# Attention b's stream: the order of VectorE, ScalarE and GpSimd within a step is taken from the source, as TensorE's already is

## The chip, the cores and the metric

The kernel runs on one core of a Trainium2 chip, in one launch. The metric is the device time of one execution in microseconds (us). The engines are named as the profile names them: PE is TensorE, DVE is VectorE, ACT is ScalarE, POOL is GpSimd, and SP is the engine that issues the DMAs.

## The reference

The input `x` is float32 of shape [2][512][512]: two batches of 512 tokens with 512 features. Four layers follow one another, each with a layer norm in front and a residual around it:

```python
x = x + attn_a(layernorm(x))   # 32 heads, 8 key heads, head size 128, int4 weights
x = x + ffn(layernorm(x))      # 8 experts of rank 64, top 2 per token   ("f1")
x = x + attn_b(layernorm(x))   # 32 heads, 8 key heads, head size 16
x = x + ffn(layernorm(x))      # the same experts again                  ("f2")
```

Attention b, cut to what matters here:

```python
q, k, v = rope(resid @ Wq), rope(resid @ Wk), resid @ Wv
att = q @ k.T / sqrt(16)                     # per head, 4 heads share a key head
att = where(causal, att, -inf)
out = softmax(att) @ v
return heads_joined(out) @ Wo
```

The experts' layer, for each token: softmax of eight gates, the two largest kept and scaled to a sum of one, and `out = sum over e of w[e] * (x @ A[e].T @ B[e].T)`.

## The kernel before, in words

The whole computation is written in a scheduling framework: the source emits instructions, and a scheduler decides in what order each engine's queue holds them, from its own estimate of when they are ready. A region `with tc.manual_schedule(engines={...})` takes this freedom away for the engines that it names: each of them issues the instructions emitted inside this region in the order of emission. The order between engines stays a matter of semaphores, and where a region's instructions fall among those of the same engine that are emitted outside it (another region too) stays the scheduler's.

The tokens of a batch are four tiles of 128 rows. `x[b, t]` stays in SBUF (`x_r` in the profile), and every residual is added in place. The layers of the two batches overlap. After attention a and the first projections, one long loop, the **stream**, does attention b for both batches (L948 to L985), and beside it, as fillers, pieces of the other layers.

**The stream's main work.** It goes over 32 pairs; a pair `p` is two heads of one batch (16 pairs a batch). Each pair takes three steps, and the second half of a pair's work follows the first by eight steps (`LEAD`), so the loop has 104 steps. Each step is a region of its own, in which only PE keeps the emitted order. In a step, in order of emission:

- `queries_halved(p + 1)`, once in four pairs: it splits a block of turned queries into a rounded part (ACT, L752) and the rest (POOL, L753), tile `hl`, and sends it through DRAM (SP, L734).
- `queries_in(p)`: SP loads the pair's queries `qs` (L761), POOL clears their extra rows (L763).
- `maxima_in(p)`: PE transposes the row maxima (`tpm`, L804), and ACT copies them into the extra rows of `qs` (L807), so that the next product comes with the maximum subtracted.
- `probabilities`: PE multiplies keys by queries (`st_b`, L828), ACT takes the exponential (`pT_b`, L834), POOL clears what lies above the diagonal (affine select, L837).
- `maxima`: PE multiplies queries by keys (`sc_b`, L781), DVE takes each row's maximum from PSUM (`top`, L785); at the end of a pair POOL splits these maxima in two parts with four small operations (`mm`, L793 and L794). The tiles are taken as (0, 1), then 3, then 2, so a tile name `sc_b_2_3_0` is pair 2, tile 3, half 0.
- `weighted_b`: PE multiplies probabilities by values (`num_b`, L854); for the last tile ACT copies the result out (L865), and DMAs send its sums.

`sc_b`, `st_b` and `tpm` share five PSUM banks (pool `ps_x`), the fillers have two (`ps_f`), and `num_b` has one. A bank comes free when DVE or ACT has read what it held.

**The fillers** are Python generators that a number called `pace` advances a little in each step, at the step's end. In the first half these are the rest of experts f1 for batch 1 and `projections(1)` (norm, keys, queries of batch 1); in the second half `output_b` (the output projection `po`, L910, with its residual, L914) and experts f2 for batch 0. A filler begins with `norm_parts` (L158): for each of the four tiles the statistics and their aggregate on DVE (`bn_stats`, L163; `bn_aggr`, L164), then the standard deviation (ACT, square root, L166), its reciprocal (DVE, L168), the normalised tiles `xn` (DVE, L173), their transposes `pxT` (PE, L178), and a copy (ACT, L179). ACT's square root and exponential have different tables, so the trace has a table load ahead of L166 and another ahead of the next exponential. All of the norm's statistics are emitted in one piece:

```python
for t in range(NT):
    st = small.tile([P, 6], F32, tag="st", name=f"st_{which}_{b}_{t}")
    nc.vector.bn_stats(st, x[b, t])
    nc.vector.bn_aggr(var[:, t, :], st)
```

Of the experts, these lines matter here: for each tile POOL spreads the gate weights (`we`, L255), PE transposes them (`wT`, L259), DVE multiplies them in (L261), and then come the products `py` (PE, L266) with the residual (DVE, L270) and the store of the output (SP, L272). `divided` (L882) turns the sums into reciprocals, loads them as a broadcast (`rb`, L897, SP), and multiplies (`oN`, L900, DVE).

After the stream the rest follows on its own: the output projection of batch 1 and experts f2 for batch 1.

Of the kernel before, what the change touches and what calls it, by code (L numbers as in the profile page):

```python
# [40 lines left out]
def kernel(  # L41
# [238 lines left out]
    with ExitStack() as actx:  # L280
# [226 lines left out]
        def chain(*stages):  # L507
            for stage in stages:
                yield from stage
# [231 lines left out]
    def keys_in(b, kh):  # L741

        if kh == 0:
            kparts[b] = spread(khls[b], f"k_{b}", (slice(0, 4, 2), slice(1, 4, 2)))
        nc.sync.dma_start(ks[kh][:HALF], kparts[b][:, ts(kh, 4), :])

    def queries_halved(p):

        b, kh, g, _ = pairs[p]
        hl = hlp.tile([P, 2, S], F32R, tag="hl", name=f"hl_{p}")  # L750
        src = qTs[b][:, kh * 2 + g // 2, :]
        nc.scalar.copy(hl[:, 0, :], src)  # L752
        nc.gpsimd.tensor_tensor(hl[:, 1, :], src, hl[:, 0, :].bitcast(F32), ALU.subtract)  # L753
        to = spread(hl, f"q_{p}", (slice(0, 2), slice(2, 4)))
        for n in range(4):
            qparts[p + n] = to

    def queries_in(p):
        _, _, g, pr = pairs[p]
        q = qs[p % NQ]  # L760
        nc.sync.dma_start(q[:HALF], qparts.pop(p)[:, ts((g % 2) * 2 + pr, 2), :])  # L761
        if p >= NQ:
            nc.gpsimd.memset(q[HALF:HM], 0.0)  # L763
# [35 lines left out]
    def maxima_in(p):  # L799

        mm = mms.pop(p).bitcast(F32)
        tp = ps_x.tile([P, S], F32, tag="x", name=f"tpm_{p}")
        for t in range(NT):
            nc.tensor.transpose(tp[:HM, ts(t, P)], mm[:, t, :], ident)  # L804
        for h in range(2):
            at = (1 - h) * HALF
            nc.scalar.copy(qs[p % NQ][HALF:HM, h, :].bitcast(F32R), tp[at : at + 2, :])  # L807
# [39 lines left out]
    def weighted_b(b, kh, g, j, pT):  # L847


        first, last = j == 0, j == NT - 1  # L850
        if first:
            nums[b, kh, g] = ps_n.tile([P, S], F32, tag="num", name=f"num_b_{b}_{kh}_{g}")
        for sp in range(4):
            nc.tensor.matmul(  # L854
                nums[b, kh, g][ts(sp, STRIP), j * P :], vpads[b][:, j, kh, sp, :], pT[sp],
                start=first, stop=last,
            )
        if not last:
            return
        c, par = kh * 2 + g // 2, g % 2  # L860
        if par == 0:
            got = oNs[b, c] = bp.tile([P, S], F32, tag="oN", name=f"oN_b_{b}_{c}", bufs=6)
        else:
            got = temps.tile([P, S], F32, tag="t", name=f"o1_b_{b}_{c}")
        nc.scalar.copy(got, nums.pop((b, kh, g)))  # L865

        row, pair = (c % 2) * 2 + par, (b, kh)
        if row == 0:
            dens[pair] = dram.tile([2, 4, 2, S], F32, tag=f"dens{kh}", name=f"dens_b_{b}_{kh}", bufs=1)
        nc.sync.dma_start(dens[pair][c % 2, :, par, :], got[B_HD:P:STRIP, :])  # L870
        if par == 1:

            for sp in range(4):
                at = sp * STRIP
                nc.sync.dma_start(oNs[b, c][at + B_HD : at + STRIP, :], got[at : at + B_HD, :])
        if row == 3:
            quotients.append(divided(b, kh))
# [25 lines left out]
    def output_b(b, cs):  # L903

        while not all((b, c) in ready for c in cs):
            yield MM
        for i in range(NT):
            po = place("bank", [P, DM], f"po_{b}_{i}_{cs[0]}")
            for c in cs:
                nc.tensor.matmul(  # L910
                    po, oNs[b, c][:, ts(i, P)], wo2[:, c, :], start=(c == cs[0]), stop=(c == cs[-1])
                )
                if c == cs[-1]:
                    nc.vector.tensor_tensor(x[b, i], x[b, i], po, ALU.add)  # L914
                yield MM

    def run(*stages):
        stages = list(stages)
        while stages:
            stages = [st for st in stages if next(st, stages) is not stages]  # L920
# [25 lines left out]
    banks[:], homes["we"] = BESIDE, (wep, "we")  # L946
    side = chain(later, projections(1))
    pace, left = 0.8, 0.0  # L948
    for step in range(total + LEAD):
        with tc.manual_schedule(engines={mybir.EngineType.PE}):  # L950
            if step == LEAD:
                pace = 0.95
            if step == half - 4:
                run(side)
                keys_in(1, 0)
                queries_halved(len(pairs) // 2)
                side = output_b(0, (0, 1))
                pace, left = 0.37, 0.0
            if step == half + LEAD:
                keys_in(1, 1)  # L960
            if step == half + LEAD + 10:
                side = chain(side, output_b(0, (2, 3)), experts(0, "f2", True))
                pace, left = 0.95, 0.0
            if step == total - 6:
                side = chain(output_b(1, (0, 1)), side)
                pace, left = 1.4, 0.0
            quotients[:] = [q for q in quotients if next(q, None) is not None]
            p, at = divmod(step + 4, STEPS)
            if at == 0 and p % 4 == 3 and p + 1 < len(pairs) and p + 1 != len(pairs) // 2:
                queries_halved(p + 1)  # L970
            if at == 0 and 2 <= p < len(pairs):
                queries_in(p)
            p, at = divmod(step - 4, STEPS)
            if at == 0 and 0 <= p < len(pairs):
                maxima_in(p)
            if LEAD <= step:
                next(ps)
            if step < total:
                next(ms)

            if len(due) > 3 and due[3][0] <= step:
                for _ in range(4):
                    weighted_b(*due.pop(0)[1])
            left += pace
            while left > 0:  # L985
                got = next(side, None)
                if got is None:
                    left = 0.0
                else:
                    left -= got  # L990
# [99 lines left out]
```

## Time and profile before

| | us |
|---|---|
| median of three runs | 1094.37 (1093.66 to 1094.58) |
| profiled execution, its own time | 1095.07 |
| its span, first to last instruction | 1093.4 |

| engine | busy, us | share of the span | instructions |
|---|---|---|---|
| PE | 1046.9 | 96% | 4940 |
| DVE | 859.0 | 79% | 2175 |
| ACT | 627.2 | 57% | 1475 |
| POOL | 598.5 | 55% | 916 |

The mean granted clock of PE is 0.992 of full speed. Times in the trace count from the span's start. The stream runs from about 792 to 1028 us. In a line of the timeline, the first number is the start, the second the duration; then come engine, source line, operation, what it writes and reads, with shapes and the count that is drawn together in this line; in square brackets stands how long the engine was idle just before, and whose work ended that wait. A weight load of PE has an engine name of its own, PEld.

### The profile page before, as it was taken

The numbers are of one execution on the slowest core, as the hardware profiler recorded it, in microseconds if no ns is written. First come the engines' busy times: TensorE is split into PE (matmuls) and PEld (weight loads), VectorE is DVE, ScalarE is ACT, GpSimd is POOL, SyncE is SP. The second block draws the span as 40 slices with busy tenths as digits, with TensorE's granted clock in tenths as the row PEclk, the third lists the DMA queues.
The fourth block names the chain that finished last, engine by engine and source line by source line (L and its number), as shares of the span: only waits on it lengthen the run. The fifth ranks groups of instructions, "written<-read, shape, count | busy, mean of one in ns | idle before, by whom it ended". The sixth has DMA issues, their size and how long they took to land.

```text
span 1093.4 us, 16248 instructions
## 1 busy us (share of the span) xinstructions
PE 1046.9 (96%) x4940; PEld 707.0 (65%) x4940; DVE 859.0 (79%) x2175; ACT 627.2 (57%) x1475; POOL 598.5 (55%) x916
## 2 busy tenths in 40 slices
PE   5799999999999999999999999999999999999988
PEld 3477767777777677777777777556467655565534
DVE  6889899999999999999999999574386667766142
ACT  3666666567666566566666665513166567685410
POOL 2466666677576666666666666262245566554200
PEclk9999999999999999999999999999999999999999
DMA  7301011012110010010021000042342235211011
GB/s 294 116 1 39 1 39 39 1 39 78 39 40 25 16 39 20 20 39 12 28 75 42 1 1 1 1 155 75 87 161 83 57 122 149 88 49 35 28 38 39
DMA packets 23271, 60.47 MB, mean 55 GB/s; under 512 B 4369, under 2 KB 5329, under 8 KB 20369
## 3 DMA queue, kind: packets, MB, share of 16 engines
q1 hardware_dynamic: 23184, 59.44, 16.4%
q8 instruction: 40, 0.66, 0.2%
q14 instruction: 47, 0.38, 0.1%
HBM read 45.53 MB, written 12.85 MB: 53 GB/s over the span
## 4 chain that ended last, share of the span: by engine, by line
PE 80%; DVE 9%; ACT 4%; issue 2%; POOL 2%; DMA 2%; SPq 0%; ACTq 0%; POOLq 0%; DVEq 0%
PE sc L412 11%; PE av L445 11%; PE tp L440 6%; PE ph_f L207 5%; PE ps_q L365 5%; PE ps_o L457 5%; PE ps_o L458 5%; PE ps_q L366 4%; PE st_b L828 4%; PE py_f L266 3%; PE sc_b L781 3%; PE num_b L854 3%; PE po L910 3%; PE pq_b L701 2%; DVE r_q L372 1%
## 5 line engine op out<-in xcount | busy, mean ns | idle before, releaser
L429 POOL TENSOR_SCALAR p<-p,rden 128x128 f32<-128x128 f32 (+3 forms) x256 | 152.4, 607 | 227.0 <-DVE rden L427 167.1
L420 ACT ACTIVATE p<-sc,nmx 128x128 f32<-128x128 f32 (+3 forms) x256 | 135.8, 530 | 110.3 <-DVE nmx L415 108.7
L412 PE MATMUL sc<-kT,qT 128*128 128x128 f32 (+3 forms) x512 | 180.5, 435 | 1.7 <-ACT p L420 1.3
L372 DVE SCALAR_TENSOR_TENSOR r_q<-ps_q,s_q,r_q 128x512 f32<-128x512 f32 x192 | 143.8, 749 | 20.6 <-PE ps_q L366 16.3
L467 DVE SCALAR_TENSOR_TENSOR acc<-ps_o,s_o,acc 128x512 f32<-128x512 f32 x186 | 137.5, 744 | 19.9 <-PE ps_o L458 17.7
L785 DVE CUSTOM_DVE_ANT_0 sc_b<-sc_b,tri 128x128 f32<-128x128 f32 (+3 forms) x256 | 119.8, 517 | 42.2 <-PE sc_b L781 27.8
L445 PE MATMUL av<-pT,v 128*128 128x512 f32 (+3 forms) x512 | 148.5, 433 | 0.0
L445 PEld LDWEIGHTS av<-pT,v 128*128 128x128 f32 x512 | 96.7, 189 | 64.2 <-issue 36.2
L415 DVE CUSTOM_DVE_ANT_0 sc<-sc,tri 128x128 f32<-128x128 f32 (+3 forms) x256 | 125.9, 492 | 11.2 <-PE sc L412 10.3
L441 ACT COPY pT<-tp 128x128 f32<-128x128 f32 (+3 forms) x256 | 108.2, 423 | 46.0 <-PE tp L440 45.6
L365 PE MATMUL ps_q<-xh,w_q 128*128 128x512 f32 x256 | 121.1, 473 | 3.0 <-ACT r_v L370 1.4
L440 PE MATMUL tp<-ident,p 128*128 128x128 f32 x640 | 114.2, 274 | 3.2 <-POOL p L429 1.6
L412 PEld LDWEIGHTS sc<-kT,qT 128*128 128x128 f32 x512 | 94.9, 189 | 27.6 <-ACT p L420 6.9
L457 PE MATMUL ps_o<-ah,w_o 128*128 128x512 f32 x256 | 110.4, 431 | 1.8 <-DVE acc L467 1.2
L366 PE MATMUL ps_q<-xl,w_q 128*128 128x512 f32 x256 | 101.6, 397 | 0.0
L458 PE MATMUL ps_o<-al,w_o 128*128 128x512 f32 x256 | 101.2, 395 | 0.0
L834 ACT ACTIVATE pT_b<-st_b 128x384 f32<-128x384 f32 (+1 forms) x192 | 89.8, 529 | 17.8 <-PE st_b L828 16.7
L440 PEld LDWEIGHTS tp<-ident,p 128*128 128x128 f32 x640 | 78.5, 140 | 31.6 <-issue 8.7
L837 POOL TENSOR_SCALAR_AFFINE_SELECT pT_b<-pT_b 128x128 f32<-128x128 f32 (+1 forms) x192 | 63.4, 339 | 63.6 <-ACT pT_b L834 59.6
L387 POOL TENSOR_TENSOR r_q<-r_q,tab 128x512 f32<-128x512 f32 x64 | 82.2, 1284 | 9.1 <-DVE rs_q L384 9.1
L465 POOL TENSOR_TENSOR acc<-acc,part 128x512 f32<-128x512 f32 x62 | 80.0, 1290 | 11.5 <-ACT part L464 11.5
L388 POOL TENSOR_TENSOR qT<-r_q,rs_q 128x512 f32<-128x512 f32 x64 | 82.6, 1291 | 5.0
(179 smaller groups left out, 2062.9 us busy)
## 6 DMA issues: line engine op xcount, KB each, us to landing
codes_q<-in_q_codes_dram SPq DMA_DIRECT2D x8, 1024.0 KB
codes_o<-in_o_codes_dram SPq DMA_DIRECT2D x8, 1024.0 KB
spread_q<-hl SPq DMA_DIRECT2D x16, 512.0 KB
qs<-spread_q SPq DMA_DIRECT2D x32, 256.0 KB
x_a<-in_x_dram SPq DMA_DIRECT2D x8, 256.0 KB
codes_k<-in_k_codes_dram SPq DMA_DIRECT2D x2, 1024.0 KB
codes_v<-in_v_codes_dram SPq DMA_DIRECT2D x2, 1024.0 KB
x_r<-in_x_dram SPq DMA_DIRECT2D x8, 256.0 KB
```

Of the source, the lines that this page charges most:

```text
L365: nc.tensor.matmul(ps, w[:, c, ts(h, A_HD)], xh[b][:, c, :], start=True, stop=False)
L366: nc.tensor.matmul(ps, w[:, c, ts(h, A_HD)], xl[b][:, c, :], start=False, stop=True)
L372: nc.vector.scalar_tensor_tensor(r, ps, s, r, ALU.mult, ALU.add)
L412: nc.tensor.matmul(sc[:, :n], qT[:, ts(i, P)], kT[:, :n], start=True, stop=True)
L415: nc.vector.tensor_tensor_reduce(sc[:, :n], sc[:, :n], tri[:, S - n :], -(A_HD**-0.5), 3e38, ALU.add, ALU.min, nmx,)
L420: nc.scalar.activation(pr, sc[:, :n], AF.Exp, bias=nmx, scale=-1.0, accum_out=den[:, i % 2 : i % 2 + 1],)
L429: nc.gpsimd.tensor_scalar(prs[j], prs[j], rden[:, j % 2 : j % 2 + 1], 1.0, ALU.mult, ALU.mult)
L440: nc.tensor.transpose(tp[:, j, :], prs[i][:, ts(j, P)], ident)
L445: nc.tensor.matmul(av[:, j * P :], v[:, j, :], pT[:, j, j * P :], start=(j == 0), stop=(j == NT - 1))
L457: nc.tensor.matmul(ps, w[:, h, ts(n, P)], ah, start=True, stop=False)
L458: nc.tensor.matmul(ps, w[:, h, ts(n, P)], al, start=False, stop=True)
L467: nc.vector.scalar_tensor_tensor(to, ps, s, to, ALU.mult, ALU.add)
```

## The change

The region of each of the 104 steps names four engines in place of one. DVE, ACT and POOL thereby keep the emitted order within a step; from step to step they stay free, as PE does. No instruction is added or taken away.

```diff
     side = chain(later, projections(1))
     pace, left = 0.8, 0.0
+    STREAM = {getattr(mybir.EngineType, e) for e in ("PE", "DVE", "Activation", "Pool")}
     for step in range(total + LEAD):
-        with tc.manual_schedule(engines={mybir.EngineType.PE}):
+        with tc.manual_schedule(engines=STREAM):
             if step == LEAD:
                 pace = 0.95
```

## The prediction

> **What bounds the kernel now.** I read the page's busy row first, then the windows over the stretch in which the change acts (about 780 to 1029 us), then the timeline wherever TensorE (PE) stands idle there.
>
> ```profile
> PE 1046.9 (96%) x4940; PEld 707.0 (65%) x4940; DVE 859.0 (79%) x2175; ACT 627.2 (57%) x1475; POOL 598.5 (55%) x916
> ```
>
> PE is busy 96% of the span; the other engines cost time only where they make PE wait. The windows' columns are length, busy time of PE, PEld, DVE, ACT and POOL with counts, granted clock, DMA share, GB/s:
>
> ```profile
> 782.00:808.00 26.00, 23.15 (x89) 12.90 (x87) 19.78 (x70) 8.55 (x14) 7.94 (x18) 1.00 0.53 173
> 806.00:808.00 2.00, 0.65 (x4) 0.41 (x3) 1.41 (x8) 1.97 (x3) 1.84 (x5) 1.00 0.01 4
> 808.00:840.00 32.00, 31.91 (x209) 23.90 (x210) 21.27 (x89) 23.25 (x55) 17.23 (x52) 0.95 0.23 71
> 809.00:812.00 3.00, 3.00 (x10) 2.31 (x10) 2.44 (x7) 2.94 (x7) 2.26 (x5) 0.50 0.93 320
> 962.00:1000.00 38.00, 35.89 (x222) 23.47 (x226) 27.14 (x117) 27.66 (x55) 18.98 (x57) 0.96 0.18 52
> 966.00:969.00 3.00, 3.00 (x15) 2.58 (x14) 1.57 (x9) 2.59 (x6) 1.27 (x4) 0.50 0.03 8
> 1000.00:1029.00 29.00, 28.96 (x184) 16.33 (x177) 7.74 (x23) 15.67 (x32) 10.85 (x35) 1.00 0.03 7
> ```
>
> In 808 to 840 and 1000 to 1029 PE is full: whatever delays it ahead of them reaches the end, as there is no idle time in which to win it back. It has spare time in two places, around 806 and 962, and behind each it runs some 3.4 us at half clock. These are the places where a layer norm's pieces meet the maxima. The timeline of the first:
>
> ```profile
> 787.98 0.70 DVE L163 BATCH_NORM_STATS2 st_b<-x_r 128x6 f32<-128x512 f32 x1
> 791.41 0.70 DVE L163 BATCH_NORM_STATS2 st_b<-x_r 128x6 f32<-128x512 f32 x1
> ...
> 805.90 1.27 POOL L753 TENSOR_TENSOR hl<-qT,hl 128x512 fp32r<-128x512 f32 x1 [0.23 <-ACT hl L752]
> ...
> 806.37 0.14 DVE L785 DVE_READ_ACCUMULATOR2_ANT top<- 128x1 f32 x1
> ...
> 807.45 1.28 ACT L834 ACT_TABLE_LOAD   x1
> ...
> 808.06 0.63 PE L804 MATMUL tpm<-ident,mm 128*66 128x128 f32 x4 [1.39 <-POOL mm L794]
> ```
>
> Two of the four statistics ran 15 to 20 us ahead, while DVE had nothing else; the third (798.68) and fourth (803.48) were slipped in later. The last maximum of pair 2 is read by 806.51; POOL splits it (four operations, 807.12 to 808.00) after the subtraction of `hl`; PE had waited 1.39 for that. Both table loads (1.28 each) ran before that, under the wait.
>
> **The change part by part.** It adds and removes no instruction, DMA or table load. A region is one step, so each engine keeps the emitted order within a step and is still free across steps. In the built queues of the two programs, SP's order is the same; the queues differ in five places.
>
> **A, second norm of attention b (802 to 818).** All four statistics pairs now stand between pair 2's maxima. Each costs 0.58 to 0.61 (start to start) and its aggregate 0.09. Before the last maximum lie four statistics and three aggregates, 4 x 0.59 + 3 x 0.09 = 2.63, where 0.76 lay before (803.39 to 804.06, and 0.09 at 804.66). Taking the one at 798.68 out of pair 1 brings the start forward some 0.2 (PE's wait for `mm` at 802.30 then binds). The maximum is ready 2.63 - 0.76 - 0.2 = 1.7 later, at 808.2. POOL's `hl` subtraction, now behind two selects, whose exps have moved ahead of ACT's `hl` copy, ends at 808.36 instead of 807.17. The four splitting operations take 0.88: 809.24, and `tpm_2` starts at 809.3 instead of 808.06, +1.24.
> Then ACT: the Exp reload moves behind the two `qs_2` copies (1.16). 809.95 + 1.16 + 1.28 = 812.4 for the next exp (`pT_0_3`), instead of 810.82. That is +1.6, and PE's matmuls after it need its PSUM banks; between them PE and DVE now hand over banks one by one, about 0.3 more. The first `num` group, 818.46 in the trace, starts at 820.35 at full clock (+1.9). But the trace already shows clock 0.50 behind a 2 us stretch with 0.65 busy, and the new stall is longer; with the half-clock stretch falling as it does now over this group's scores I reach 821.5, **+3.0**, and take that. Bounds: +1.2 (`tpm_2` alone, all else hidden), and +4.7 (a second half-clock stretch: 3.4 us at half speed do 1.7 us of work).
>
> One page speaks to the reload. The Trainium skill, "ScalarE: Activation LUTs", section What ACT_TABLE_LOAD costs, puts a switch of tables at 1283 ns plus about 1380 ns of drain. The trace shows the load, 962.99 to 964.27, and the next exp at 964.28, so 1.28 and no drain; by the page the reload would add 1.38 more, and A would be +4.4.
>
> **B, the norm of experts f2, batch 0 (958 to 971).** Before, the statistics are at 945.13, 950.18, 953.00 and 959.16; the last delays pair 25's maxima, and PE waits:
>
> ```profile
> 960.80 0.73 PE L781 MATMUL sc_b<-ks,qs 128*128 128x512 f32 x2 [0.69 <-DVE top L785]
> ...
> 964.83 0.33 PE L781 MATMUL sc_b<-ks,qs 128*128 128x128 f32 x1 [0.43 <-ACT pT_b L834]
> 965.32 0.61 PE L781 MATMUL sc_b<-ks,qs 128*128 128x128 f32 x3 [0.16 <-ACT pT_b L834]
> 966.38 1.06 PE L804 MATMUL tpm<-ident,mm 128*66 128x128 f32 x4
> ```
>
> Now all four stand between pair 25's maxima. They start about 0.6 earlier (the 959.16 one gone), a reciprocal and small waits leave (0.5), 2.63 comes in: 963.90 + 2.63 - 0.6 - 0.5 = 965.4. Half of the splitting follows, so `tpm_25` comes at about 966.0, which is 0.4 before the trace's 966.38, as `pxT_0` no longer precedes it. The two table loads, now on either side of the `qs_0` copies, put the next exp at 966.6 + 1.16 + 1.28 = 969.05 against 968.66; `xn` and the transposes `pxT_0`, `pxT_1` (0.35 each) come behind it. The `num` group at 970.52 starts at 970.5 at full clock (0), at 971.7 with the half-clock stretch the trace has here: **+1.2**. Bounds: -0.7 (the 0.69 wait goes and all else hides) and +2.0 (+1.7 of half clock on +0.3).
>
> **C, the end of the stream (1024 to 1030).** GpSimd's copies `we_0`, `we_1` (L255, 0.61 each) ran early, at 999.77 and 1000.71. They now come behind the selects of `pT_31`, and the transposes `wT` on PE need them:
>
> ```profile
> 1024.36 0.67 POOL L837 TENSOR_SCALAR_AFFINE_SELECT pT_b<-pT_b 128x128 f32<-128x128 f32 x2 [0.38 <-ACT pT_b L834]
> 1024.64 0.60 PE L259 MATMUL wT_f<-ident,we_f 128*128 128x128 f32 x4
> 1025.31 0.61 POOL L255 COPY we_f<-gw_f 128x512 f32<-128x512 f32 x1 [0.27 <-PE wT_f L259]
> ...
> 1026.07 2.36 PE L854 MATMUL num_b<-pT_b,vpad 128*32 128x512 f32 x32
> ```
>
> `we_0` ends at 1025.0 + 0.6 = 1025.6, so `wT_0` starts at 1025.65 instead of 1024.64. `we_1` stands behind the two 0.4 selects at 1027.04 and ends at about 1027.95. `num`, 1028.43 at its end, ends at 1029.55: **+1.1** (0.4 if PE finds other matmuls, 1.2 at most: two copies). From here the chain PE, `py`, residual, store, broadcast DMA (1037.50, SP), multiply, output has no slack, as SP issues that DMA 0.43 behind a store that itself waits for `py`.
>
> **D, pair 21 (933 to 938).** The multiply L900 (0.75) moves ahead of a maximum; behind it, at 934.62, it delayed the next ones and PE waited 0.84 at 937.74. Half of the multiply comes back, **-0.35**; -0.7 if all. If the broadcast `rb` (issued 928.64; landing 4.3 later where I could follow one, 873.9 to 878.2) comes late, DVE waits with the maxima behind it: up to +0.7.
>
> **E, some 17 swaps on POOL, a few of ACT.** Two selects of 0.29 now precede the four splitting operations instead of lying between them. The last operation ends at the same time: **0** (cover: the same four operations; 0.3 either way).
>
> Sum: 3.0 + 1.2 + 1.1 - 0.35 = +4.95. The traced execution took 1095.07 (span 1093.4); the median of three, 1094.37, is 0.7 lower, and no row of the change depends on that. Applied to the median: **1099.3**.
>
> **The rivals.** First, **faster**: B's waits from 960.8 to 965.5 (0.69 + 0.17 + 0.21 + 0.21 + 0.43 + 0.16 = 1.87) go and D gives 0.35, while A's statistics are hidden because POOL's `hl` subtraction, not DVE, sets `mm`. 1094.37 - 2.2 = 1092.1. It is decided at `tpm_2`: only if PE waits no more than 1.4 there. Against it stands that DVE is the later one by my sum by 0.9 of work, and that `hl` itself comes later. 0.13.
> Second, **almost nothing**: order within a step is so little that only `tpm_2`'s 1.2 and C's 0.4 arrive, B is 0, D -0.35: +1.25, 1095.6. For it: only 30 or so instructions move across a wait. This is also the case in which the change does less than its name. 0.20.
> Third, **a second half-clock stretch** at each norm: 4.7 + 2.0 + 1.2 - 0.35 = +7.55, 1101.9. For it: the trace grants half clock behind stretches with 0.65 of 2 us busy. 0.20.
> On this a rule can be set beside the rows. The trace has the longest wait ahead of half clock at 1.39. The Trainium skill, "TensorE: Matmul & The Clock Gate", Part 1: The HAM clock gate, says that half rate comes after at least one idle window of about 3.4 us. By it neither place would be throttled, and with the full-clock ends 1.9 + 0 + 1.1 - 0.35 the sum would be +2.65, 1097.0; the rows already contradict it.
>
> **How the numbers follow.** The forecast has 0.47. What this kernel's measurement can tell from no change is about 0.2%, 2.2 us. Faster by more than that: the first rival, 0.13. Within it: the second, 0.20. Slower: forecast and third, 0.67. The range: up to the third rival with D at its bad end (1101.9 + 1.05 = 1103.0), down to 1092.8, which leaves the better half of the first out.
>
> **What would show it.** Right: pair 2's last maximum near 808.2, `tpm_2` with a wait above 2 us, an Exp reload behind the `qs_2` copies; the 960.80 wait gone, but half clock still there; `wT_0` at about +1.0 beyond the shift until then. The first `num` group, the one at 970.52 and the one at 1026.07 give A, A + B + D and all but C. Wrong: PE busy as before at 806 to 812, half-clock stretches that vanish or double, or idle time of PE at a step where no order differs.

## The result, and the profile after

The changed kernel takes 1105.32 us (median of four, 1100.32 to 1108.01) against 1094.01 (four, 1092.57 to 1094.58): a ratio of 1.0112 [1.0092, 1.0133], or 12.2 us. It is slower, at the places that the prediction named, and by more than twice the forecast of +4.95; 1105.32 lies above the range as well. The profiled execution took 1100.32 with a span of 1098.5. It is the fastest of nine executions of this program in two batches (1100.32 to 1108.01), so it understates the change: its trace tells where time goes, the ratio how much.

The page's busy row of the changed kernel:

```profile
PE 1048.8 (95%) x4940; PEld 705.9 (64%) x4940; DVE 858.7 (78%) x2175; ACT 627.0 (57%) x1475; POOL 598.0 (54%) x916
```

The work is the same, to within 2 us on PE. What changes is where PE waits and how fast it may run. Its windows, columns as before (length; busy time of PE, PEld, DVE, ACT, POOL; granted clock; DMA share; GB/s):

```profile
...
806.00:809.20 3.20, 0.94 (x4) 0.59 (x4) 3.20 (x15) 2.60 (x5) 2.52 (x7) 0.90 0.01 3
808.00:840.00 32.00, 29.58 (x168) 21.53 (x172) 19.94 (x83) 20.39 (x46) 16.09 (x49) 0.84 0.21 67
808.60:818.80 10.20, 9.04 (x33) 6.86 (x33) 4.96 (x22) 6.05 (x12) 3.82 (x13) 0.50 0.38 129
...
968.80:970.80 2.00, 0.09 (x2) 0.01 (x1) 2.00 (x12) 1.38 (x2) 0.94 (x5) 1.00 0.03 8
...
1000.00:1029.00 29.00, 28.55 (x156) 15.81 (x155) 11.96 (x50) 15.96 (x33) 9.07 (x33) 1.00 0.03 6
```

Read the long ones against their counterparts of before. In 808 to 840 PE does 168 matmuls where it did 209, at a mean clock of 0.84 where it was 0.95. Ahead of that, DVE is busy through all of 806.0 to 809.2 while PE has 0.94; behind it PE is held at half clock for 10.2 us, where it was 3.4. The same comes at 968.8: DVE full, PE with 0.09 of 2.00, and 3.4 us of half clock from 972.4. Between 1000 and 1029 PE is full again: what has been lost by then reaches the end.

The timeline at the first place shows DVE's queue and what hangs on it:

```profile
803.27 0.69 DVE L163 BATCH_NORM_STATS2 st_b<-x_r 128x6 f32<-128x512 f32 x1
...
806.98 0.66 DVE L163 BATCH_NORM_STATS2 st_b<-x_r 128x6 f32<-128x512 f32 x1
807.11 1.26 POOL L753 TENSOR_TENSOR hl<-qT,hl 128x512 fp32r<-128x512 f32 x1 [0.23 <-ACT hl L752]
...
808.02 0.14 DVE L785 DVE_READ_ACCUMULATOR2_ANT top<- 128x1 f32 x1
...
809.25 1.06 PE L804 MATMUL tpm<-ident,mm 128*66 128x128 f32 x4 [2.07 <-POOL mm L794]
...
811.53 1.28 ACT L834 ACT_TABLE_LOAD   x1
```

All four statistics (803.27, 804.57, 805.84, 806.98) now lie among pair 2's maxima. The last maximum is read by 808.16, POOL's subtraction ends at 808.37, and `tpm_2` starts at 809.25 after a wait of 2.07 instead of 1.39. The Exp table is now loaded behind the `qs_2` copies (1.16), at 811.53 where it was 807.45; the exp follows at 812.83.

At the end of the stream, the copies `we` stand behind POOL's selects:

```profile
1031.13 0.61 POOL L255 COPY we_f<-gw_f 128x512 f32<-128x512 f32 x1
...
1031.80 0.66 PE L259 MATMUL wT_f<-ident,we_f 128*128 128x128 f32 x4 [0.57 <-POOL we_f L255]
1032.50 1.69 PE L854 MATMUL num_b<-pT_b,vpad 128*32 128x512 f32 x10
...
1033.58 1.16 POOL L255 COPY we_f<-gw_f 128x512 f32<-128x512 f32 x2
1034.24 0.66 PE L259 MATMUL wT_f<-ident,we_f 128*128 128x128 f32 x4
1034.83 1.50 PE L854 MATMUL num_b<-pT_b,vpad 128*32 128x384 f32 x22
1036.38 0.58 ACT L865 COPY o_b<-num_b 128x512 f32<-128x512 f32 x1 [3.22 <-PE num_b L854]
```

Of the copies, which had run at 999.77 and 1000.71, the first now starts at 1031.13 and the next two at 1033.58. PE waits 0.57 for the first, and the second set of transposes now cuts the last `num` group in two.

### The profile page after: what moved, and what is told of

It reads as the page before. It is cut to its first block, busy times and chain, and to the rows that moved or that the text cites. A ratio compares the mean times of both kernels' runs of the same rounds, so it can differ in the third digit from the quotient of the medians.

```text
span 1098.5 us, 16259 instructions
## 1 busy us (share of the span) xinstructions
PE 1048.8 (95%) x4940; PEld 705.9 (64%) x4940; DVE 858.7 (78%) x2175; ACT 627.0 (57%) x1475; POOL 598.0 (54%) x916
## 4 chain that ended last, share of the span: by engine, by line
PE 80%; DVE 9%; ACT 4%; POOL 2%; issue 2%; DMA 1%; SPq 0%; ACTq 0%; POOLq 0%; DVEq 0%
PE sc L412 11%; PE av L445 11%; PE tp L440 6%; PE ph_f L207 5%; PE ps_q L365 5%; PE ps_o L457 5%; PE ps_o L458 5%; PE ps_q L366 5%; PE py_f L266 4%; PE st_b L828 3%; PE num_b L854 3%; PE sc_b L781 3%; PE pq_b L701 2%; PE po L910 2%; DVE r_q L372 1%
## 5 line engine op out<-in xcount | busy, mean ns | idle before, releaser
L465 POOL TENSOR_TENSOR acc<-acc,part 128x512 f32<-128x512 f32 x62 | 79.9, 1288 | 11.5 <-ACT part L464 11.5
```

## The experiments

The theory from the prediction: the four statistics of a norm, held between a pair's maxima, delay `tpm`, and half clock follows; this is worth most of the 12 us. Rivals: the cost lies in many small waits of the rest; or it lies in what comes after the statistics. Except where a diff says otherwise, a kernel differs from the changed one only in the steps, or engines, that keep the emitted order. In these diffs a minus line is the changed kernel's, and

```diff
+    PE_ONLY = {mybir.EngineType.PE}
```

comes with those that name it. Steps 6 and 75 hold the statistics of the two norms, with the deviation and its reciprocal, which are emitted in the same piece ("statistics" below means all of these); steps 7 to 12 and 76 to 82 hold the rest of the norms (`xn`, `pxT`, copies). "us" below is (ratio - 1) times the kernel before of the same batch (medians 1092.2 to 1093.3, of 15 to 30 runs).

**again**: the changed kernel unchanged.

> The changed kernel once more, unaltered. Clock theory: behind pair 2's late maxima PE is so little busy in one 3.4 us window that a chain of half-clock windows starts, and its length depends on where the windows fall in that execution; the times scatter again over 1100 to 1108, and the longer ones have the lower mean clock (0.984 to 0.991). Waits alone: all executions lie within 1 us of the first profiled one's 1100.3, whatever the clock.

Measured: 1.0112 [1.0093, 1.0130], +12.2 us; median of five 1104.97, profiled span 1101.6. The size stands. In the windows view of this execution the half-clock stretch behind `tpm_2` is longer than in the first, with the same order on each engine:

```profile
807.60:821.20 13.60, 11.86 (x43) 9.37 (x44) 8.27 (x35) 8.87 (x17) 6.21 (x18) 0.50 0.28 102
```

13.6 us instead of 10.2: the length of half clock is not fixed by the program.

**free6** and **only6**: the first norm's statistics alone set free, and alone held.

```diff
-        with tc.manual_schedule(engines=STREAM):
+        with tc.manual_schedule(engines=STREAM if step != 6 else PE_ONLY):   # free6
+        with tc.manual_schedule(engines=STREAM if step == 6 else PE_ONLY):   # only6
```

> All four engines in order in every step but step 6, in which only PE is (there the norm of projections(1) is emitted, so its statistics run ahead again). Clock theory: nearly all of the loss is behind that norm; 1095 to 1097, little scatter, clock 0.991 or above. Waits spread over the stream: 1099 or more, since only the 1.2 us at the transposes of pair 2 come back.

> The kernel before, with all four engines in order in step 6 alone. Clock theory: it has nearly the whole loss, 1100 to 1106, and the scatter. Waits spread over the stream: 1096 or less (1.2 to 1.9 us).

Measured: free6 1.0076 [1.0054, 1.0097], +8.3; only6 1.0036 [1.0021, 1.0050], +3.9. So step 6 counts for about 4 us from either side: a third of the total, and close to A's +3.0. Two thirds lie elsewhere.

**fill**: the changed kernel with four products that nobody reads, at the end of step 9, right before `tpm_2`, so that PE isn't idle there.

```diff
+            if step == 9:
+                idle = place("bank", [P, DM], "idle_9")
+                for n in range(4):
+                    nc.tensor.matmul(idle, ident, wq2[:, n % NC, :], start=(n == 0), stop=(n == 3))
```

> The changed kernel with four more 128x512 products on PE, which nobody reads, right ahead of pair 2's transposes (about 1.9 us at full clock, in the 2.07 us in which PE stood idle). Clock theory: with PE busy there the half-clock windows do not start, and the time falls by 4 us or more, to 1096 to 1099, though PE does more. Waits alone: no gain, 0 to 0.5 us slower than the changed kernel.

Measured: 1.0078 [1.0062, 1.0093], +8.5. The timeline and the windows of fill:

```profile
807.39 3.60 PE L995 MATMUL idle<-wq,ident 128*128 128x512 f32 x8
...
822.29 1.93 PE L854 MATMUL num_b<-pT_b,vpad 128*32 128x512 f32 x20
```

```profile
807.40:821.00 13.60, 11.84 (x59) 7.57 (x58) 9.66 (x38) 10.36 (x19) 7.03 (x18) 1.00 0.32 115
```

The products overshoot the idle time, so `tpm_2` comes 1.58 later than in the changed kernel (810.83 against 809.25). Even so the `num` group starts at 822.29, earlier than 823.50, since the clock is at full. Without the 1.58 it would be 820.7; the prediction's full-clock figure was 820.35. The kernel gains 3.7 us on **again** in spite of the products. So half clock at A costs some 2.8 us in these traces (823.50 - 820.7).

**only75** and **free6_75**: the second norm's statistics alone held; both norms' statistics alone set free.

```diff
-        with tc.manual_schedule(engines=STREAM):
+        with tc.manual_schedule(engines=STREAM if step == 75 else PE_ONLY):           # only75
+        with tc.manual_schedule(engines=STREAM if step not in (6, 75) else PE_ONLY):  # free6_75
```

> The kernel before, with all four engines in order in step 75 alone (where the norm of experts f2 is emitted). Theory of the second norm: B was mis-sized, since in the profiles of the changed kernel and of the one with step 6 freed the shift grows by 1.8 to 3.3 us between the transposes of pairs 24 and 27; with the half-clock windows 3 to 6 us slower than before. Rival, the forecast's size: 1.2 us, and the missing 5 us lie in C, D and E.

> All four engines in order in every step but 6 and 75: what stays is C, D and E. Theory of the second norm: within 2 us of before. Rival: 4 us or more slower.

Measured: only75 1.0019 [1.0004, 1.0034], +2.1; free6_75 1.0094 [1.0071, 1.0118], +10.3. Here the theory begins to fail. Held alone, the two steps cost 3.9 + 2.1 = 6.0; set free out of the whole, they give back only 12.2 - 10.3 = 1.9. The two differences are known to about 2.3 and 3.3 us, so this alone does not settle it; it suggests that something else takes their place as the delay.

**dve** and **no_dve**: order kept in all steps, but by PE and DVE alone, or by PE, ACT and POOL.

```diff
-    STREAM = {getattr(mybir.EngineType, e) for e in ("PE", "DVE", "Activation", "Pool")}
+    STREAM = {getattr(mybir.EngineType, e) for e in ("PE", "DVE")}                 # dve
+    STREAM = {getattr(mybir.EngineType, e) for e in ("PE", "Activation", "Pool")}  # no_dve
```

> Only PE and DVE are held in order, ACT and POOL are free. In its queues the two norms' statistics stand where the changed kernel has them, and the square roots and table loads follow them; the gate copies of C run early, as before. Theory that the place of the statistics costs the time: nearly the whole loss, 9 to 12 us. Rival, that ACT's and POOL's order costs it: 1 to 4 us.

> PE, ACT and POOL are held in order, DVE is free: the statistics stand where they stood before, C and E are as in the changed kernel. Theory of the statistics: 0 to 2 us slower than before. Rival (ACT's and POOL's order): 6 us or more.

Measured: dve 1.0070 [1.0051, 1.0088], +7.7; no_dve 1.0039 [1.0024, 1.0054], +4.3. Together 12.0, which is the whole: the two add, DVE's order bears two thirds, ACT's and POOL's one third. Part of that third has a place in the timeline that I had priced at nothing. From no_dve, ahead of a `pq` product of batch 1:

```profile
837.93 0.87 ACT L834 ACTIVATE pT_b<-st_b 128x384 f32<-128x384 f32 x2 [0.74 <-PE st_b L828]
838.69 0.34 ACT L681 COPY vpad<-pkv_b 128x64 f32<-128x64 f32 x2
839.08 1.13 PE L701 MATMUL pq_b<-wq,xnT_b 128*128 128x512 f32 x2 [0.28 <-ACT vpad L681]
```

and from the kernel before, ACT at the same work:

```profile
836.43 0.27 ACT L151 CAST khl<-tpk 128x128 fp32r<-128x128 f32 x1 [0.50 <-PE tpk L666]
836.66 0.87 ACT L834 ACTIVATE pT_b<-st_b 128x384 f32<-128x384 f32 x2
```

Before, ACT took the cast while it waited for a score, then the exponentials. In order, it waits 0.74 for the score first, and the copies that free the fillers' banks come behind: PE waits 0.28 for `vpad`. The stream has 16 `num` groups, numbered from 0 in order of time; from the start of group 0 to that of group 2 it now takes 29.76 (819.13 to 848.89) instead of 28.69 (818.46 to 847.15). The half with this wait grows by 0.47 (14.29 to 14.76); the other, 14.40 to 15.00, by 0.60 without a wait of PE that the profile lists, and which copy holds it up is not shown. The stretch is 29.74 to 29.77 in all nine profiles in which ACT and POOL keep order there, and 28.68 to 28.71 in all others.

**seg_norm1**, **seg_mid**, **seg_norm2**, **seg_end**: the changed kernel in four pieces, one at a time.

```diff
-        with tc.manual_schedule(engines=STREAM):
+        with tc.manual_schedule(engines=STREAM if 6 <= step <= 12 else PE_ONLY):    # seg_norm1
+        with tc.manual_schedule(engines=STREAM if 13 <= step <= 74 else PE_ONLY):   # seg_mid
+        with tc.manual_schedule(engines=STREAM if 75 <= step <= 82 else PE_ONLY):   # seg_norm2
+        with tc.manual_schedule(engines=STREAM if step >= 83 else PE_ONLY):         # seg_end
```

> All four engines in order in steps 6 to 12 alone: the first norm with its statistics (step 6) and its normalised tiles and transposes (steps 10 to 12). Sum of pieces (the loss is made of four pieces of 1 to 4 us each, of which I had sized only some): 3 to 4.5 us slower than before. One piece with the whole of the missing time elsewhere: 3.2 as with step 6 alone, and then one of the other three is at 5 us or more.

> All four engines in order in steps 13 to 74 alone: E with the key projections' copies and subtractions (L151, L152) behind the exponentials and maxima, and D. Sum of pieces: 1 to 2 us slower than before, since the shift of num grows by 1.1 us between groups 0 and 2 wherever ACT is held in order (the changed kernel, its repeat and the one without DVE's order), and by nothing where it is not. Forecast's size: -0.35.

> All four engines in order in steps 75 to 82 alone: the second norm with its normalised tiles and transposes. Sum of pieces: 2.5 to 4 us slower (2.2 for step 75 alone, and in the profile of the kernel with steps 6 and 75 freed the shift still grew by 3.3 here). One piece: 5 us or more. Forecast's size: 1.2.

> All four engines in order from step 83 on: C. Sum of pieces: 1.5 to 2 us slower (profiles with C take 66.0 to 66.7 us from the last num group to the end, those without it 64.5 to 64.9, the kernel before's 67.3 apart, which has a half-clock window there). Forecast's size: 1.1.

Measured: 1.0037 [1.0022, 1.0052], +4.0; 1.0013 [1.0000, 1.0025], +1.4; 1.0025 [1.0013, 1.0038], +2.7; 1.0003 [0.9990, 1.0015], +0.3. The sum is 8.4, where the whole is 12.2. Each piece is known to about 1.5 us, so four of them to about 3: the gap is at the edge of what this can tell. The two norms come first in size, and the first norm's whole (4.0) is no more than its statistics alone (3.9).

**both_norms** and **free_norms**: the two norms' steps held together, and everything but them.

```diff
-        with tc.manual_schedule(engines=STREAM):
+        with tc.manual_schedule(engines=STREAM if 6 <= step <= 12 or 75 <= step <= 82 else PE_ONLY):  # both_norms
+        with tc.manual_schedule(engines=PE_ONLY if 6 <= step <= 12 or 75 <= step <= 82 else STREAM):  # free_norms
```

> All four engines in order in steps 6 to 12 and 75 to 82 alone. Sum of pieces: about 6.7 us slower than before (4.0 and 2.7). Joint effect: 9 us or more.

> All four engines in order in every step but 6 to 12 and 75 to 82, so that statistics, normalised tiles and transposes of both norms stand free. Sum of pieces: about 1.7 us slower than before (1.4 and 0.3 for the middle and the end alone). Joint effect: 5 us or more.

Measured: both_norms 1.0068 [1.0053, 1.0083], +7.4; free_norms 1.0031 [1.0018, 1.0044], +3.4. Together 10.8 against 12.2: within the intervals the norms and the rest add up. The first part is as large as DVE's order alone (7.7), the second about as large as ACT's and POOL's (4.3).

**tiles_only**: of the norms' steps, those without statistics.

```diff
-        with tc.manual_schedule(engines=STREAM):
+        with tc.manual_schedule(engines=STREAM if 7 <= step <= 12 or 76 <= step <= 82 else PE_ONLY):
```

> All four engines in order in steps 7 to 12 and 76 to 82 alone: the statistics stand where they stood before, and the normalised tiles, their transposes and copies stand behind the maxima and exponentials. Theory that either delays the same chain: 5 to 8 us slower than before, as with the statistics held too (7.4). Theory of the statistics: 2 us or less.

Measured: 1.0054 [1.0036, 1.0072], +5.9. With the statistics free, holding the rest of the norms costs as much as holding the statistics alone (6.0), and both together 7.4, not 11.9 (a gap of 4.5, known to about 3.4). So the two do not add up, and the theory that the statistics are the cost falls. The timeline of tiles_only at the second norm says what is late here:

```profile
970.14 0.54 DVE L173 TENSOR_SCALAR xn_f<-x_r,mv_f,rstd_f 128x512 f32<-128x512 f32 x1
...
972.53 1.05 PE L178 MATMUL pxT_f<-ident,xn_f 128*128 128x128 f32 x4
```

against the kernel before:

```profile
963.76 1.00 DVE L173 TENSOR_SCALAR xn_f<-x_r,mv_f,rstd_f 128x512 f32<-128x512 f32 x2
```

The normalised tile comes at 970.14, behind maxima, where two had come from 963.76 on, between them; the whole stream is 2.95 late by then (`num` group 10), so 3.4 of this is new. PE has `pxT` at a place of its own and gets to it only at 972.53: a second way to delay the same stretch. In its windows view 6.80 us at half clock follow, from 969.20.

**after_fill** and **before_fill**: is it half clock that costs, at every place? Unread products at the idle places of the changed kernel, and of the kernel before (there against the kernel before's own code). The steps are chosen from the idle times in the traces:

```diff
+            if step == 40:    # likewise: after_fill 9 (4 products), 66 (2), 78 (4); before_fill 9 (3), 66 (1), 76 (1), 78 (1), 3 before the last output projection
+                idle = place("bank", [P, DM], "idle_40m")
+                for n in range(3):
+                    nc.tensor.matmul(idle, ident, wq2[:, n % NC, :], start=(n == 0), stop=(n == 2))
```

> The changed kernel with PE's idle stretches filled with 128x512 products that nobody reads: four ahead of pair 2's transposes, three where the maxima wait for a DMA (step 40), two ahead of pair 21's transposes, four ahead of pair 25's. Clock theory (about half of the loss is half-clock windows that the deeper stretches set off, a varying number of them): mean clock 0.995 or more, 3 to 8 us faster than the changed kernel though PE does 5.6 us more, and the executions closer together. Waits alone: no gain, and 0 to 3 us slower.

> The kernel before with the same kind of products in its own idle stretches: three ahead of pair 2's transposes, three in step 40, one ahead of pair 21's transposes, one each in steps 76 and 78, three ahead of the last output projection. Clock theory: its half-clock windows (in its profile four in and behind the stream) go, mean clock 0.997, 1 to 4 us faster than before, so faster than both kernels. Waits alone: 0 to 3 us slower.

Measured: after_fill 1.0105 [1.0089, 1.0121], +11.5, clock 0.998 in its profile; before_fill 1.0002 [0.9993, 1.0012], clock up to 1.0. Neither tells what half clock costs, as the products take time too. In **after_fill** they overshoot the idle time by 1.4 at step 9, 1.5 at step 40, 0.75 at step 66 and 1.5 at step 78. In **before_fill** `tpm_2` comes 1.0 later (16.45 behind the stream's first `sc_b`, where it was 15.43). At step 40 the products cost as much as half clock did: from `num` group 4 to 5 the kernel before takes 13.45 with its half-clock stretch and **before_fill** 13.92 without, while **only75**, **seg_end** and **seg_norm2**, which have the kernel before's order up to there and no half clock in that stretch, take 12.3 to 12.6.

**before_fit**: the kernel before with smaller products, to fit its idle time; it was also the version that might have beaten both.

```diff
+            if step == 66:    # likewise 76; 9 and 40 with 512 columns; one of each before the last output projection
+                idle = place("bank", [P, DM], "idle_66")
+                nc.tensor.matmul(idle[:, :256], ident, wq2[:, 0, :256], start=True, stop=True)
```

> The kernel before with products in five idle stretches of PE, this time sized to fit: one of 128x512 of these takes 0.86 us, not the 0.43 I had counted, so that the earlier fillings overshot the idle time (by 1.2 us each ahead of pair 2's transposes and in step 40). Now 0.86 ahead of pair 2's transposes, 0.86 in step 40, 0.43 ahead of pair 21's transposes, 0.43 in step 76, 1.29 ahead of the last output projection. Clock theory: the half-clock windows still go, nothing is delayed, and the time falls by 2 to 3.5 us, below both kernels. Rival, the windows lie in time that is spare anyway: no change within 0.5 us.

Measured: 0.9999 [0.9987, 1.0010], -0.1 us. No version of these beats the kernel before. The stretch at step 40 still takes 13.53. That half clock costs the kernel before nothing is not shown by this: of its 106 executions measured beside these experiments, the 21 with a mean clock of 0.996 or more have a median of 1091.1, the 29 with 0.992 or less 1093.9. This shows that low clock and a longer time go together, not which brings which.

## Why the prediction was right and wrong

**Direction and place: right.** It said slower with 0.67, by way of the two norms, and the norms bear 7.4 of the 12.2.

**The first rival (faster)** was to be decided at `tpm_2`, with a wait of no more than 1.4. It is 2.07: the rival fell there. **The second (almost nothing)** fell too. **The third** (a second half-clock stretch, +7.55) came nearest, still 4.6 short.

**A, +3.0 (1.2 to 4.7): the place right, half clock mis-sized.** Its steps hold to 0.1: maximum 808.2 (808.16), `hl` 808.36 (808.37), `tpm_2` 809.3 (809.25), next exp 812.4 (812.83, the one step off by 0.4, since `tpm_2` takes 1.06 at half clock instead of 0.63, and the copies follow it; the exp starts as the table load of 1.28 ends, at 811.53 + 1.28 = 812.81, with no drain). One reading of the kernel before was off, though no term rests on it: its second table load ran from 807.45 to 808.73, not wholly ahead of `tpm_2` at 808.06. The first norm's steps, held alone, measure 4.0 [2.4, 5.7]; in the traces the first `num` group is 4.7 late (table below). What I had mis-sized was half clock. I took one stretch of 3.4 us; the trace has three in a row, and four in **again**. The first `num` group starts at 823.50 instead of 821.5, and **fill** shows why, as it is at about 820.7 with full clock. One window follows another:

```profile
805.14:808.55 3.41, 1.56 (x6) 0.89 (x6) 3.41 (x15) 2.88 (x5) 2.27 (x5) 1.00 0.01 2
808.56:811.97 3.41, 2.72 (x10) 1.95 (x10) 1.23 (x7) 1.66 (x4) 1.21 (x4) 0.50 0.81 300
...
815.38:818.79 3.41, 3.33 (x16) 2.60 (x14) 1.63 (x8) 2.20 (x6) 1.58 (x7) 0.50 0.00 0
```

The first has PE at 1.56 of 3.41 and is followed by half clock; the next two at half clock still have gaps (2.72 here, 2.99 in the one left out), and half clock goes on; the one that PE fills (3.33) ends it.

The Trainium skill, "TensorE: Matmul & The Clock Gate", Part 1: The HAM clock gate, asks for at least one idle window of about 3.4 us before half rate. The length of a window agrees with these 3.41; the condition doesn't, as no idle time here is longer than 2.07. Its consequence in the prediction, +2.65 in all, is further from 12.2 than the forecast.

**B, +1.2 (-0.7 to 2.0): the term that was mis-sized.** Steps 75 to 82 alone measure 2.7 [1.4, 4.2]. What I worked out was there: the timeline of the changed kernel has `tpm_25` at 970.79, 4.41 after 966.38, where the shift had been 4.85 at the `num` group before: 0.4 early, as forecast. The `num` group that I used as my end stands at 976.18, a shift of 5.66, so +0.8. But I stopped at that group. The rest of the norm comes behind it:

```profile
970.79 0.63 PE L804 MATMUL tpm<-ident,mm 128*66 128x128 f32 x4 [1.91 <-POOL mm L794]
...
976.18 2.36 PE L854 MATMUL num_b<-pT_b,vpad 128*32 128x512 f32 x32
982.26 0.66 PE L178 MATMUL pxT_f<-ident,xn_f 128*128 128x128 f32 x4
983.94 1.06 PE L197 MATMUL pg_f<-xnT_f,gw 128*32 128x512 f32 x8
```

against the kernel before:

```profile
974.13 0.60 PE L178 MATMUL pxT_f<-ident,xn_f 128*128 128x128 f32 x4
...
976.17 1.06 PE L197 MATMUL pg_f<-xnT_f,gw 128*32 128x512 f32 x8
```

The last four transposes come 8.13 later than there, and the first product that needs them 7.77, where the `num` group was 5.66 late. Two groups on (1005.49 against 999.34) the shift is 6.15, so B makes +1.3 in this execution. It is a short one: from `num` group 10 to 13 it takes 45.7, and the seven profiles with DVE in order through that norm take 45.4 to 48.0, 2.6 more on the mean than the seven with DVE free there.

**The step that failed in both norms** is that I hung the cost on the statistics. Holding them (6.0) and holding what follows from them (5.9) delays the same stretch of PE, and both together cost 7.4. I costed what the statistics push back on DVE; I did not follow `xn`, `pxT` and the copies, which PE has at fixed places, as a chain of their own. The traces put the overlap at the second norm. At the first, the statistics alone delay `num` group 0 by 2.6 (**only6**) and the rest alone by 1.1 to 2.3 (**free6_75**, **free6**, **tiles_only**), which about adds up to the 4.7 of both. At the second, the stretch from group 10 to 13 grows by 1.8 with the statistics alone (**only75**) and by 3.3 and 4.5 with the rest alone (**free6_75**, **tiles_only**), more than the 2.6 of both.

**E, 0 (either way 0.3): wrong by 1.06**, in every profile with that order. I said that the same four POOL operations cover the swaps, and treated the "few of ACT" along with them. On ACT no such cover exists: a copy that had used a wait now stands behind it, and the fillers' banks come free later. In the trace PE's wait for that is 0.28; that the rest of the 1.06 has the same cause is not shown.

**C, +1.1 (0.4 to 1.2): the place was right, the size too small by the traces.** In the changed kernel's trace the shift grows by 1.75, from 6.14 at `num` group 14 to 7.89 at the copy that ends `num` (1036.38 against 1028.49). PE waits 0.57 for the first copy, and the other one comes in the midst of `num`. That stretch takes 15.62 to 15.63 in all nine profiles with this order, and 13.87 to 13.88 in the other eleven. Behind it, both sorts take 62.0 to 62.8 to the end, but for the kernel before (64.9, with a half-clock stretch there) and **before_fill** (63.4). Yet alone C measures +0.3 [-1.1, 1.6], and why so little of the 1.75 shows there stays open.

**D, -0.35: half clock left out.** The stretch from `num` group 8 to 10 takes 26.04 in the changed kernel and 26.05 in **again**, against 26.34: -0.3, as forecast. But in four other profiles with that order (**free6**, **dve**, **seg_mid**, **free_norms**) a half-clock window falls in it, and it takes 27.4 to 27.8. No profile without that order has one there. On the mean of these profiles D costs 0.8.

**The sum.** The terms as measured by the pieces are 4.0 + 2.7 + 1.4 + 0.3 = 8.4; norms and rest give 10.8; engines give 12.0; the whole is 12.2. The twenty profiles, one execution each, say more about the places than these sums. In the table, order means DVE's at A, D and B, and ACT's and POOL's at E and C; profiles with unread products in the stretch are left out of A, B and D:

| stretch | order free there | order kept there | more on the mean | forecast |
|---|---|---|---|---|
| A: the stream's first `sc_b` to `num` group 0 | 25.6 to 25.9 (7 profiles) | 30.1 to 31.1 (5) | 4.7 | 3.0 |
| E: group 0 to 2 | 28.68 to 28.71 (11) | 29.74 to 29.77 (9) | 1.06 | 0 |
| D: group 8 to 10 | 25.7 to 26.3 (9) | 26.0 to 27.8 (8) | 0.8 | -0.35 |
| B: group 10 to 13 | 43.1 to 45.3 (7) | 45.4 to 48.0 (7) | 2.6 | 1.2 |
| C: group 14 to the copy that ends `num` | 13.87 to 13.88 (11) | 15.62 to 15.63 (9) | 1.75 | 1.1 |

Together 10.9: so most of the 12.2 has a place, and the forecast of 4.95 was short at every one of them. The remaining 1.3 is within what the intervals allow.

I had worked out one path with one stretch of half clock at fixed places. The first profile shows such a lucky execution, its span longer by only 5.1 us; the other eight executions of the program took 2.1 to 7.7 us more than this one. The range needed that spread at its upper end. Of the 3.1 us between its two traced executions 2.4 arise at a place for which the prediction has no term, between `num` groups 4 and 5: there the first profile takes 12.27 and so wins back 1.2 on the kernel before (13.45), though I had held that nothing is won back; **again** takes 14.66. In **again** DVE's multiply L900, with maxima behind it, starts at 887.73 instead of 886.53 behind a wait for a DMA (its broadcast is issued at 881.29 and 881.36), PE waits 2.37 instead of 1.10, and half clock follows at 889.5. Over the profiles without unread products at that place, this stretch takes 12.3 to 13.2 without half clock (6) and 13.4 to 14.7 with it (11).

**Still open:** what the half-clock stretches at B cost in the changed kernel (**after_fill** overshoots there), and whether a change of the emitted order itself, with `xn` and copies placed ahead of the maxima, would keep the order at no cost; that was not tried.

## What to carry to other kernels

When an engine is held to the emitted order, follow each of the work's chains, not only the first operation that is late: a side stream of norm, normalised tile, transpose and copy delays PE as surely by its last link as by its first, and taking one delay away leaves the other. An engine at 57% busy is not free to be ordered: its idle time lies in waits, and a small copy that used such a wait can end up behind it. And count on a spread: where half clock and the landing of a DMA fall differently from one execution to the next, one trace is a sample, and the fastest of nine here was 4.6 us below their median.

## What the runs showed of the hardware

Half-clock stretches in the stream last whole multiples of 3.41 us (3.4, 6.8, 10.2 and 13.6 were seen). They can follow a window of that length in which PE is partly idle, with no idle time over 2.07 in it: 1.56 of 3.41 busy in the changed kernel, as shown above, and 2.01 in the kernel before, ahead of the half clock at 809:

```profile
805.57:808.98 3.41, 2.01 (x14) 1.56 (x13) 2.82 (x14) 3.35 (x5) 2.04 (x6) 1.00 0.27 100
```

These runs give no limit of busy time for it. In the changed kernel the window from 1057.73 has 1.96 of 3.41 busy, and full clock goes on. At half clock, the one from 972.39 ended the stretch with 2.84 busy, and in **again** the one from 814.42 did not end it with 3.33.

How many there are differs between executions of one program: mean clock 0.984 to 0.992 over nine executions of the changed kernel. Filling the idle time with unread products raises the clock to 0.995 to 1.0 in the kernel before, and the time stays (1.0002 [0.9993, 1.0012] and 0.9999 [0.9987, 1.0010]); as the products take time themselves, this does not show half clock to be free there.

A product with 512 columns of plain f32 operands is drawn as two records and took 0.86 us on PE (8 records, 3.44 from 807.39 to 810.83), so four of them overshot an idle time of 2.07.
